# A graph transformer on one core: three low-degree blocks moved to the end of the first layer, one more packing of slots, longer early parts

## The chip, the core and the metric

The kernel runs on one core of a Trainium2 chip. The metric is device time in microseconds of one launch. In the program text the two layers are numbered 0 and 1; the description of the change numbers them 1 and 2, so that its "layer 1" is layer 0 here.

## The reference

Two layers of a typed graph transformer over 6250 nodes of 128 features, 100000 edges, 16 node types and 32 edge types, then a linear map, a residual and a layer norm. Cut to what matters:

```python
def gt_layer(x, ntype, etype, src, dst, Wk, Wq, Wv, Wa, Watt, Wmsg, pri, skip, g, b):
    k, q, v = (typed_linear(x, ntype, W).reshape(n, H, HS) for W in (Wk, Wq, Wv))
    kT = jnp.einsum('nhd,htdo->nhto', k, Watt)      # a row for each node and edge type
    vT = jnp.einsum('nhd,htdo->nhto', v, Wmsg)
    kw, m = kT[src, :, etype], vT[src, :, etype]
    a = jnp.einsum('ehd,ehd->eh', kw, q[dst]) * pri[:, etype].T / SQRT_D
    att = edge_softmax(a, dst, n)
    hag = jax.ops.segment_sum((m * att[:, :, None]).reshape(-1, H * HS), dst, n)
    h = jax.nn.silu(typed_linear(hag, ntype, Wa))
    alpha = jax.nn.sigmoid(skip[ntype])[:, None]
    h = h * alpha + x * (1.0 - alpha)
    return layernorm(h) * g + b
h = x
for l in range(2):
    h = gt_layer(h, ...)                             # weights of layer l
return _layernorm(x + h @ ff_w + ff_b)
```

## The kernel before, in words

**The table.** For each layer the kernel writes a table in HBM with a row for each node and edge type: 32 rows of 256 floats (128 of `kT`, 128 of `vT`) a node. The table of layer 0 is written in the first 600 us. The table of layer 1 is made from the results of layer 0, while layer 0 is still running.

**Blocks and slots.** Nodes are sorted by class (four classes of four node types) and degree, and put 128 at a time, one a partition, into 49 blocks. A block has a width: the number of slots, which is the largest degree that its nodes may have (`OWN` for the eleven blocks of a class, `SHARED` for five blocks that take what is left over from all classes). A **gather** (line 1801, `kv<-tab,ell`) is one indirect DMA on POOL's queue; it brings for each of the 128 nodes the table row of one edge: 128 rows of 1 KB. So a layer costs about as many gathers as its blocks have slots.

**Riding slots.** The last slots of the widest blocks are used by few nodes. Where a slot's upper lanes (partitions) are unused, another slot's few lanes are gathered into them: the rider's indices are copied into the host's index column beforehand, and after the host's gather a small DMA on SP's queue (`kv<-kv`) copies the lanes back down to the rider's own place. A riding slot costs no gather. Before the change a rider and its host lie in the same block.

**Superblocks and visits.** Three or four blocks form a superblock: of each class c, `ca` is the four widest blocks, `cb` the middle four, `cc` the three narrowest; `+a` and `+b` are the shared ones. A visit is the gathers, scores, softmax and sums of one superblock. `ORDERS` gives the order of the visits in each layer. After a visit of layer 0 its **chain** (normalise, typed linear, layer norm, key and value of the next layer) and its **pieces** run beside the gathers of later visits: pieces are the matmuls against the edge weights, the copies into one of three buffers `st`, and the **puts**, one indirect DMA on POOL's queue for each half block (line 2023, `tab<-st,row`), 128 rows of 16 KB, 2.1 MB. A superblock of four blocks has eight puts, one of three has six; layer 1's table takes 98.

**What sets the order.** POOL's instructions stand in the order in which the program emits them. While it emits the gathers, it advances generators by a `tick` a slot: `spread` gives a generator of some steps a rate, so that it ends after a given number of slots. The chain's rate comes from `pace`, that of the pieces from the last lines of `table`. A finished `st` waits some steps and is put when at least three gathers (`APART`) have passed. The other engines' order is set by a scheduler within the data's dependencies.

**Early parts.** Layer 1 cannot gather rows that are not yet put. Its first two visits (the leads, `1a` and `2a`) are therefore split: an early part, whose gathers (`ells` in the names) take only edges whose sources are in superblocks put earlier, and a rest, gathered after the last put. `LATE = (2, 1)` says that the early part of the first lead leaves out the last two superblocks of layer 0's order, and that of the second lead the last one; `EARLY` says how many slots of each block are early. So the first early gather has to see the landing of all puts but those of the last two superblocks, the first of the second lead (before it the pieces of the superblock before the last are rushed to their end) all but those of the last one, and the first gather of the rest has to see the landing of the last put.

**The ring.** Gathers land in a ring of 50 slots; VectorE multiplies and reduces them from there.

## Time and profile before

| what | us |
|---|---|
| time, median of three runs (lowest to highest) | 2882.24 (2880.25 to 2885.86) |
| the profiled execution's own time | 2874.6 |
| its span | 2872.7 |
| first gather of layer 0 / first early gather of layer 1 / first gather of the rest (start) | 595.58 / 1738.71 / 1875.91 |
| last gather / last output write on POOL (start) | 2801.20 / 2864.37 |
| gathers, puts, output writes on POOL | 1620, 98, 49 |

The page of the profile gives each engine's busy time and then the span in 40 equal slices of 71.8 us. The slices up to the eighth are the preparation and layer 0's table, slices 9 to 26 layer 0's edges beside layer 1's table, and those after it layer 1's edges. POOL's busy time is only the issuing of DMAs. The transfers are in the DMA row. In a timeline row the number in brackets is the time that the engine sat idle ahead of the instruction and what ended that idle time.

### The profile page before, as it was taken

What the parts mean: (1) busy time and instruction counts of PE and PEld (TensorE: products, weight loads), DVE (VectorE), ACT (ScalarE), POOL (GpSimd) and SP (SyncE); (2) the same over time, 40 slices, a digit from 0 to 9 for tenths busy, and PEclk for the clock granted to TensorE, in tenths of its full rate; (3) what the DMA queues carried; (4) which work ended last, traced back from release to release, by engine and by line L of the source; (5) the groups of instructions that cost most, each with busy time, mean ns of one, the idle gap of its engine ahead of it and who ended that gap; (6) DMA issues with size and microseconds to landing.
All of it is one profiled execution on the core that took longest, in us unless ns stands there. A gap on an engine that the chain in (4) does not pass through costs nothing. (4 is left out here: it accounts for less than half of the span.)

```text
span 2872.7 us, 22109 instructions
## 1 busy us (share of the span) xinstructions
PE 1729.2 (60%) x5415; PEld 750.8 (26%) x5415; DVE 1856.5 (65%) x4245; ACT 942.6 (33%) x1727; POOL 1979.3 (69%) x2118
## 2 busy tenths in 40 slices
PE   5999889834966886787687787502533433212122
PEld 2445444411322342232233222101212211111010
DVE  8358322247877775767676655747877787666663
ACT  4876655511433433344343454201111111101000
POOL 5333665557777777777777776667777777777776
PEclk9989776655675666677577776555656656555555
DMA  7999999988768777787777899863333333333331
GB/s 220 403 421 373 385 400 405 403 252 209 239 234 281 259 268 249 256 317 272 268 267 263 298 351 357 297 189 104 105 104 104 106 104 105 106 105 105 106 105 50
DMA packets 186099, 678.23 MB, mean 236 GB/s; under 512 B 55586, under 2 KB 101328, under 8 KB 160912
## 3 DMA queue, kind: packets, MB, share of 16 engines
q0 software_dynamic: 113248, 636.05, 62.2%
q1 hardware_dynamic: 66612, 37.21, 4.9%
q10 hardware_dynamic: 6096, 3.43, 0.6%
q8 instruction: 46, 0.75, 0.1%
q14 instruction: 97, 0.79, 0.1%
HBM read 254.44 MB, written 421.89 MB: 235 GB/s over the span
## 5 line engine op out<-in xcount | busy, mean ns | idle before, releaser
L1801 POOL DMA_INDIRECT kv<-tab,ell x1454 | 1386.4, 953 | 470.4 <-issue 370.6
L1817 DVE TENSOR_TENSOR kv<-kv,tb 128x768 f32<-128x768 f32 (+10 forms) x274 | 261.9, 958 | 460.8 <-DMA kv<-tab,ell 301.7
L319 PE MATMUL nb<-xm,weights 128*128 128x384 f32 (+2 forms) x640 | 361.8, 720 | 271.4 <-DVE xm L302 264.2
L361 ACT COPY st<-tb 128x1024 f32<-128x1024 f32 x376 | 368.4, 1012 | 376.7 <-PE tb L377 216.7
L350 ACT COPY st<-tb 128x512 f32<-128x512 f32 x676 | 347.4, 611 | 169.6 <-PE tb L343 90.8
L377 PE MATMUL tb<-bdv,kvT 32*128 32x512 f32 x784 | 284.4, 910 | 122.4 <-ACT st L361 108.4
L377 PE MATMUL tb<-bdk,kvT 32*128 32x512 f32 x784 | 301.0, 915 | 48.6 <-ACT st L361 40.6
L343 PE MATMUL tb<-bdv,vT 32*128 32x512 f32 x784 | 287.6, 803 | 37.7 <-ACT st L350 32.4
L319 PEld LDWEIGHTS nb<-xm,weights 128*128 128x128 f32 x640 | 160.0, 268 | 483.0 <-DVE xm L302 272.6
L1822 DVE TENSOR_REDUCE a<-kv 128x48 f32<-128x768 f32 (+10 forms) x274 | 259.5, 950 | 1.0
L1145 POOL DMA_INDIRECT tab<-st,rows x98 | 101.2, 1033 | 193.1 <-ACT st L350 152.8
L1601 DVE TENSOR_TENSOR tb<-kv,tb 128x512 f32<-128x512 f32 (+7 forms) x407 | 225.7, 555 | 2.0
L343 PE MATMUL tb<-bdk,kT 32*128 32x512 f32 x784 | 213.7, 798 | 1.7 <-DVE last_at L638 1.1
L327 PE MATMUL nb<-ident,hag 128*128 128x128 f32 x98 | 26.5, 414 | 310.3 <-DVE hag L1858 310.3
L1801 POOL DMA_INDIRECT kv<-tab,ells x166 | 159.3, 960 | 69.3 <-issue 44.8
L1590 DVE TENSOR_TENSOR kv<-kv,tb 128x768 f32<-128x768 f32 (+8 forms) x266 | 197.3, 758 | 0.8
L348 DVE COPY st<-tb 128x512 f32<-128x512 f32 x108 | 74.6, 691 | 183.0 <-PE tb L343 99.3
L302 DVE SCALAR_TENSOR_TENSOR xm<-ntb,nb 128x512 f32<-128x512 bf16 (+2 forms) x224 | 126.9, 593 | 49.2 <-PE nb L327 37.3
L343 PEld LDWEIGHTS tb<-bdv,vT 32*128 32x128 f32 x784 | 111.4, 224 | 134.5 <-ACT st L350 111.3
L377 PEld LDWEIGHTS tb<-bdv,kvT 32*128 32x128 f32 x784 | 79.4, 249 | 243.3 <-ACT st L361 185.0
L1574 ACT ACTIVATE tb<-a 128x136 f32<-128x136 f32 (+15 forms) x108 | 30.0, 278 | 312.0 <-DVE a L1572 259.4
L377 PEld LDWEIGHTS tb<-bdk,kvT 32*128 32x128 f32 x784 | 82.6, 249 | 189.0 <-ACT st L361 149.7
(405 smaller groups left out, 2286.6 us busy)
## 6 DMA issues: line engine op xcount, KB each, us to landing
kv<-tab,ell POOLq DMA_INDIRECT x1454
weights<-looks SPq DMA_DIRECT2D x40, 128.0 KB
hr<-xrd SPq DMA_DIRECT2D x16, 256.0 KB
kv<-tab,ells POOLq DMA_INDIRECT x166
xrd<-xr POOLq DMA_DIRECT2D x10, 256.0 KB
weights<-looks SPq DMA_DIRECT2D x40, 64.0 KB
hrd<-hs SPq DMA_DIRECT2D x8, 256.0 KB
hr<-xrd SPq DMA_DIRECT2D x10, 192.0 KB
```

The source lines that it names most:

```text
L302: nc.vector.scalar_tensor_tensor(xm[:, :n], ntb[:, :n], float(t), hT[:, :n], op0=ALU.is_equal, op1=ALU.mult)
L319: nc.tensor.matmul(ps[:, :n], w[:, t, :], xm[:, :n], start=(t == types[0]), stop=(t == types[-1]))
L343: nc.tensor.matmul(pt[:, b], yT[s, i * P:(i + 1) * P], bd[s, tt, :], start=True, stop=True)
L350: nc.scalar.copy(to, pt)
L361: copy(to, pt)
L377: nc.tensor.matmul(pt[:, b], yT[s, i * P:(i + 1) * P], bd[s, tt, :], start=True, stop=True)
L1145: put = nc.gpsimd.indirect_dma_start(out=tabs[0].rearrange("(n t) c -> n (t c)", t=16), out_offset=bass.IndirectOffsetOnAxis(ap=rows1[:, t ...
L1590: nc.vector.tensor_tensor((v_[:, k0:k1] if j or k0 else acc[:, :k1]) .rearrange("p k (h d) -> p k h d", h=H), v_[:, k0:k1].rearrange("p k ...
L1601: nc.vector.tensor_tensor(to, v_, to, op=ALU.add)
L1801: get = nc.gpsimd.indirect_dma_start(out=to.bitcast(I32) if l else to, out_offset=None, in_=tabs[l][:], in_offset=bass.IndirectOffsetOnAxi ...
L1817: nc.vector.tensor_tensor(kk, kk, q[:lanes].unsqueeze(1).to_broadcast([lanes, c, D]), op=ALU.mult)
L1822: nc.vector.tensor_reduce(a[:lanes, j0:j1, :], kk.rearrange("p k (h d) -> p k h d", h=H), axis=AX.X, op=ALU.add)
```

## The change

- Layer 0's order: `2c` (three blocks of 13, 12 and 11 slots) is moved from the ninth place to the last. The last two superblocks are now `0b` and `2c`, where they were `3b` and `0b`. Layer 1's order is the same.
- `EARLY` has 40 and 52 slots, where it had 32 and 44: 92 in all, where there were 76.
- The shared superblock `+b` has widths 16, 15 and 9, where it had 17, 15 and 14, and its three riders may lie in another block than their hosts: `SEATS` lists for each rider the pieces of lanes and where they ride. It gathers 37 slots a layer, where it gathered 40. A rider whose host is in an earlier block takes its place in the ring when the host is gathered (`seat`, `invite`), and waits there for its own block.
- The pieces of the last two superblocks are spread over `TAIL` = 11 slots a block (44 for `0b`, 33 for `2c`), where it was over the 32 and 44 early slots. The last chain but one is no longer sped up to 0.7 of its slots. The rule that spreads the other pieces is unchanged, but it takes the slots of the visit two places later, which is another one now.

```diff
-SHARED = (41, 20, 17, 15, 14)
+SHARED = (41, 20, 16, 15, 9)
-ORDERS = ("1c 3c 1a 1b +a 2a 0c 2b 2c 0a +b 3a 3b 0b",
+ORDERS = ("1c 3c 1a 1b +a 2a 0c 2b 0a +b 3a 3b 0b 2c",
           "1a 2a 0c 3c +b 0b 1c +a 2b 2c 3a 3b 1b 0a")
-EARLY = ((11, 8, 7, 6), (14, 11, 10, 9))
+EARLY = ((13, 10, 9, 8), (16, 13, 12, 11))
+TAIL = 11.0
-OWN_TAILS = {0: ((23, 76, 1, 52),)}
-SHARED_TAILS = {0: ((27, 58, 2, 35), (28, 48, 10, 8)), 2: ((15, 88, 1, 40),),
-                4: ((8, 64, 1, 64), (7, 84, 4, 11))}
+SEATS = {
+    "a": (((0, 24), ((0, 23, 76, 52),)),),
+    "+a": (*(((0, 29 + r), ((0, 27, 58 + 35 * r, 35),)) for r in range(2)),
+           *(((0, 31 + r), ((0, 28, 48 + 8 * r, 8),)) for r in range(10))),
+    "+b": (((1, 14), ((0, 15, 64, 35),)),
+           ((2, 7), ((0, 15, 99, 29), (1, 13, 105, 6), (2, 6, 96, 32))),
+           ((2, 8), ((1, 13, 111, 15),))),
+}
...
             def pace(v):
                 v = min(v, len(visits) - 1)
-                share = 0.7 if 2 < v < n0 else 1.0
+                share = 0.7 if 2 < v < n0 - 1 else 1.0
...
                     spread(pieces, gen, 8 * visits[v][1][1] + (4 if v else 4 + HELP),
-                           (1.0 if v + 4 < n0 else 0.5 if v + 2 < n0 else 1.0) *
-                           slots(min(v + 2, first1 - 1)))
+                           (1.0 if v + 4 < n0 else 0.5) * slots(v + 2) if v + 2 < n0 else
+                           TAIL * visits[v][1][1])
...
+                        def invite():
+
+                            for to in hosting:
+                                awaits[to] = seat(1)
+                                places[to] = awaits[to][1][:, 0, :]
+                            for b2 in range(b, i0 + k):
+                                for slot, (_, pieces) in riders.get(b2, {}).items():
+                                    for at_, n, hb, hs, lane_ in pieces:
+                                        if hb == b:
+                                            nc.sync.dma_start(places[b2, slot][at_:at_ + n],
+                                                              places[b, hs][lane_:lane_ + n])
```

POOL's instructions around the first early gather: before (`st_11536` is the last put of `3a`, `st_11590` and `st_11624` are the first two of `3b`), and now (`st_11600` is the eighth and last of `3b`).

```order
L1801 DMA kv_5794<-tab0_63,ell_77 128x256 x3
L2023 DMA tab1_64<-st_11536,row2_83 12544x4096
L1801 DMA kv_5794<-tab0_63,ell_77 128x256 x4
L2023 DMA tab1_64<-st_11590,row2_83 12544x4096
L1801 DMA kv_5794<-tab0_63,ell_77 128x256 x7
L2023 DMA tab1_64<-st_11624,row2_83 12544x4096
L1801 DMA kv_5794<-tab1_64,ells_5809 128x256 x5
```

```order
L1832 DMA kv_5795<-tab0_63,ell_77 128x256 x3
L2069 DMA tab1_64<-st_11439,row2_83 12544x4096
L2069 DMA tab1_64<-st_11467,row2_83 12544x4096
L1832 DMA kv_5795<-tab0_63,ell_77 128x256 x3
L2069 DMA tab1_64<-st_11498,row2_83 12544x4096
L1832 DMA kv_5795<-tab0_63,ell_77 128x256 x2
L2069 DMA tab1_64<-st_11538,row2_83 12544x4096
L1832 DMA kv_5795<-tab0_63,ell_77 128x256 x3
L2069 DMA tab1_64<-st_11557,row2_83 12544x4096
L1832 DMA kv_5795<-tab0_63,ell_77 128x256 x3
L2069 DMA tab1_64<-st_11600,row2_83 12544x4096
L1832 DMA kv_5795<-tab1_64,ells_5810 128x256 x13
```

The puts of layer 1's table that stand ahead of the early parts have moved closer together, since `3b`'s eight puts now go with the 36 gathers of `2c`, at half of these; and the put whose landing the first early gather has to see is now the instruction just ahead of it. Before, it was `st_11536`, with eleven gathers and two puts in between.

POOL from the end of the first lead's early part to the rest: before (the 17 gathers are the last ten of the first lead and the first seven of the second; `st_11801` is the last put of `3b`, `st_12192` the last of all, and 90 is the rest of both leads), and now (`st_11973` is the last put of `0b`, `st_12176` the last of all, and 88 is 14 early gathers and 74 of the rest).

```order
L2023 DMA tab1_64<-st_11801,row2_83 12544x4096
L1801 DMA kv_5794<-tab1_64,ells_5809 128x256 x17
L2023 DMA tab1_64<-st_11988,row2_83 12544x4096
...
L1801 DMA kv_5794<-tab1_64,ells_5809 128x256 x5
L2023 DMA tab1_64<-st_12192,row2_83 12544x4096
L1801 DMA kv_5794<-tab1_64,ells_5809 128x256 x90
```

```order
L1832 DMA kv_5795<-tab1_64,ells_5810 128x256 x5
L2069 DMA tab1_64<-st_11870,row2_83 12544x4096
L1832 DMA kv_5795<-tab1_64,ells_5810 128x256 x8
L2069 DMA tab1_64<-st_11918,row2_83 12544x4096
L2069 DMA tab1_64<-st_11973,row2_83 12544x4096
L1832 DMA kv_5795<-tab1_64,ells_5810 128x256 x16
L2069 DMA tab1_64<-st_12049,row2_83 12544x4096
...
L1832 DMA kv_5795<-tab1_64,ells_5810 128x256 x3
L2069 DMA tab1_64<-st_12176,row2_83 12544x4096
L1832 DMA kv_5795<-tab1_64,ells_5810 128x256 x88
```

The second lead's first gather (the first of the 16) now stands right behind the two last puts of `0b`, where ten gathers lay in between. Behind the last put of all stand 14 early gathers, where there were none.

More of the change, by code (lines that the diff above doesn't have):

```diff
@@ L147 @@
     OWN0, SHARED0 = CB * P, NC * CB * P
-    def riders(k, groups):
-        out, lanes = [], [P] * k
-        at = max(main for main, _, _, _ in groups) + 1
-        for main, first, n, rest in groups:
-            assert n * rest + first <= P
-            lanes[main] = first
-            for g in range(n):
-                out.append((at, rest, main, first + g * rest))
-                lanes[at] = rest
-                at += 1
-        assert at == k and all(a >= b for a, b in zip(lanes, lanes[1:]))
-        return out, lanes
-    tails = {c * CB + i: riders(OWN[i], g) for c in range(NC) for i, g in OWN_TAILS.items()}
-    tails.update({NC * CB + i: riders(SHARED[i], g) for i, g in SHARED_TAILS.items()})
     holds = slots_for(OWN, BINS, LOW)
@@ L171 @@
             named[f"{c}{part}"] = (c * CB + CB - i0 - k, k, range(c * TC, (c + 1) * TC))
+    riders, lanes_of = {}, {}
+    for name, (i0, k, _) in named.items():
+        seats = SEATS.get(name if name[0] == "+" else name[1], ())
+        if not seats:
+            continue
+        for i in range(k):
+            lanes_of[i0 + i] = [P] * KB[i0 + i]
+        taken = set()
+        for (i, slot), pieces in seats:
+            at, mine = 0, []
+            for hi, hs, lane, n in pieces:
+                assert hi <= i and (hi, hs) not in dict(seats) and lane + n <= P
+                assert taken.isdisjoint((hi, hs, lane + r) for r in range(n))
+                taken.update((hi, hs, lane + r) for r in range(n))
+                of = lanes_of[i0 + hi]
+                of[hs] = min(of[hs], lane)
+                mine.append((at, n, i0 + hi, hs, lane))
+                at += n
+            lanes_of[i0 + i][slot] = at
+            riders.setdefault(i0 + i, {})[slot] = at, mine
+    for b, of in lanes_of.items():
+        assert all(p >= q for p, q in zip(of, of[1:]))
+    hosts = {}
+    for b, of in riders.items():
+        for slot, (_, pieces) in of.items():
+            first = min(hb for _, _, hb, _, _ in pieces)
+            if first < b:
+                hosts.setdefault(first, []).append((b, slot))
     orders = [[named[part] for part in order.split()] for order in ORDERS]
@@ L1739, in edges @@
                     a = ep.tile([P, max(KB), H], F32, name="a")
-                    riding = {} if part else {k: r for k, *r in tails.get(b, ((), ()))[0]}
-                    places, halves = {}, None
-                    bundled = bundles_of(K, riding)
+                    riding = {} if part else riders.get(b, {})
+                    hosting = () if part else hosts.get(b, ())
+                    halves = None
+                    guests = {at[1]: awaits.pop(at) for at in list(awaits) if at[0] == b}
+                    places = {at: held[1][:, 0, :] for at, held in awaits.items()}
+                    bundled, main = bundles_of(K, riding, hosting)
                     stages = [bundled]
@@ L1762, in edges @@
                                     k0, pos = k0 + size, pos + size
-                            bundles += [cut] if riding and len(bundle) > 1 else [[c] for c in cut]
+                            if bundle is main:
+                                pos += len(hosting)
+                                whole.append(len(bundles))
+                            bundles += [cut] if bundle is main else [[c] for c in cut]
                             chunks += cut
```

48 lines of the change are left out of this document (28 added, 20 removed).

## The prediction

> **What bounds the kernel now.** I read the page first, then POOL's groups, its busy time by stretch, its waits, and its timeline around the layers' boundary. The page's busy shares alone don't name the bound; the groups and the stretches do.
>
> ```profile
> PE 1729.2 (60%) x5415; PEld 750.8 (26%) x5415; DVE 1856.5 (65%) x4245; ACT 942.6 (33%) x1727; POOL 1979.3 (69%) x2118
> ```
>
> ```profile
> L1801 POOL DMA_INDIRECT kv<-tab,ell x1454 | 1386.4, 953 | 470.4 <-issue 370.6 <-DMA tab<-st,rows 15.8 <-DMA kv<-tab,ell 11.6
> L1801 POOL DMA_INDIRECT kv<-tab,ells x166 | 159.3, 960 | 69.3 <-issue 44.8 <-DMA tab<-st,row 17.1 <-DMA kv<-tab,ells 2.6
> ...
> L2023 POOL DMA_INDIRECT tab<-st,row x98 | 100.6, 1026 | 36.5 <-issue 20.8 <-ACT st L361 10.6 <-DMA kv<-tab,ell 3.2
> ```
>
> Most of POOL's idle time is "issue", waiting for nothing: each DMA is followed by some 0.30 us before the next. Busy and gap together, POOL is full:
>
> ```profile
> 1600.00:1738.00 138.00, 113.05 (x332) 39.23 (x332) 81.71 (x166) 73.10 (x98) 100.40 (x105) 0.70 0.90 336
> 1738.00:1791.00 53.00, 38.31 (x110) 14.08 (x109) 32.56 (x75) 24.67 (x37) 35.12 (x37) 0.66 0.97 369
> 1791.00:1876.00 85.00, 47.45 (x156) 14.79 (x154) 60.95 (x100) 21.05 (x33) 53.08 (x56) 0.58 0.84 298
> ...
> 2400.00:2500.00 100.00, 31.80 (x71) 14.96 (x71) 66.71 (x153) 11.19 (x28) 75.82 (x80) 0.62 0.37 106
> ```
>
> (Columns: length, then busy time and count of PE, weight load, VectorE, ScalarE, POOL; granted clock, DMA share, GB/s.) In layer 1 there are 80 gathers in 100 us, **1.25 us each**, with the DMA at 0.37 and VectorE at two thirds: the issuing is the bound. A put costs 1.03 + 0.30 = 1.33 us of POOL. From 1600 to 1738 POOL's 100.40 + 105 x 0.30 leave 6.1 us of real stall; from 1738 to 1791 6.8; from 1791 to 1876 15.1. So 28 us of stalls stand where layer 1's table is finished. After that POOL runs on to the end without a break, and so a microsecond saved or lost on POOL anywhere behind 595 us reaches the end one to one:
>
> ```profile
> 2289.84 0.94 POOL L1801 DMA_INDIRECT kv<-tab,ell  x1 [1.41 <-DVE tb L1590]
> ...
> 2801.20 0.95 POOL L1801 DMA_INDIRECT kv<-tab,ell  x1 [0.30 <-issue]
> 2802.45 1.02 POOL L2079 DMA_INDIRECT out_dram<-weights,node  x1 [0.30 <-issue]
> ...
> 2864.37 0.98 POOL L2079 DMA_INDIRECT out_dram<-st,node  x1 [0.30 <-issue]
> ```
>
> The row at 2289.84 is the longest stall that I find after 1876. The stalls before it, in the timeline:
>
> ```profile
> 1636.28 1.02 POOL L2023 DMA_INDIRECT tab<-st,row  x1 [0.30 <-issue]
> ...
> 1647.21 0.94 POOL L1801 DMA_INDIRECT kv<-tab,ell  x1 [1.04 <-DMA tab<-st,row]
> ...
> 1735.38 0.95 POOL L1801 DMA_INDIRECT kv<-tab,ell  x1 [0.30 <-issue]
> 1737.39 1.01 POOL L2023 DMA_INDIRECT tab<-st,row  x1 [1.07 <-DMA kv<-tab,ell]
> 1738.71 1.03 POOL L1801 DMA_INDIRECT kv<-tab,ells  x1 [0.30 <-issue]
> ...
> 1776.26 1.01 POOL L2023 DMA_INDIRECT tab<-st,row  x1 [0.30 <-ACT th L1907]
> ...
> 1790.80 0.94 POOL L1801 DMA_INDIRECT kv<-tab,ells  x1 [4.67 <-DMA tab<-st,row]
> ...
> 1806.56 1.01 POOL L2023 DMA_INDIRECT tab<-st,row  x1 [3.57 <-ACT st L361]
> ...
> 1862.82 1.01 POOL L2023 DMA_INDIRECT tab<-st,row  x1 [0.30 <-issue]
> 1875.91 0.97 POOL L1801 DMA_INDIRECT kv<-tab,ells  x1 [12.08 <-DMA tab<-st,row]
> ```
>
> At 1875.91 the first gather of the rest waits for the last put to land: 12.08 us. The idle at 1647.21 and 1790.80 is on the eighth issue behind the puts at 1636.28 and 1776.26: eight issues last 10 us, and a put that takes longer to land holds up the eighth issue behind it. So puts here land 10.6, 14.2 and 12.8 us after their start (the idle ends about 0.3 us ahead of the gather). The first early gather (1738.71) waits for nothing: the put that it has to see is eleven gathers and two puts back.
>
> ```profile
> 1700.00:1737.00 37.00, 31.73 (x111) 10.75 (x111) 15.13 (x22) 22.93 (x27) 24.28 (x26) 0.78 1.00 391
> 1737.00:1777.00 40.00, 34.22 (x102) 11.48 (x98) 21.14 (x36) 22.22 (x29) 28.54 (x29) 0.69 0.97 377
> 1804.00:1808.00 4.00, 2.63 (x12) 0.52 (x8) 3.88 (x6) 1.44 (x3) 1.14 (x2) 0.50 0.04 16
> 1808.00:1813.00 5.00, 2.46 (x12) 0.89 (x16) 3.85 (x6) 2.02 (x2) 3.78 (x5) 0.50 1.11 410
> ```
>
> Where puts are close together, the DMA engines are full, at 377 to 391 GB/s. The put of 1806.56 met idle engines: its data began to flow 1.4 us after its start, at 410 GB/s.
>
> **The change, part by part.**
>
> *Gathers.* The order has 1614 gathers in place of 1620 (three a layer, all of `+b`), and the same 98 puts and 49 output writes. 6 x 1.25 = **-7.5 us**. On POOL's path this is certain; nothing hides it. The 16 early slots that are added are gathers moved from the rest, and save nothing by themselves.
>
> *Pieces riding in another block.* `+b` now has five such small copies a layer on SP's queue, where it had six. SP takes its queue in order, so behind a copy that waits for its host's gather stand the loads of `hr`, `ntb` and the stores of `hrd`. VectorE waits for a copied slot before the guest's scores. What hides this is the ring: POOL runs up to 50 slots (62 us) ahead of VectorE. I take 0. Only if VectorE fell that far behind would it cost; the row at 2289.84 (1.41 us) is the nearest price, so 0 to +2. The six issues of these copies before were in the same queue, so there is no gain to expect either.
>
> *The dense stretch and the first early gather.* `3b`'s pieces are spread over half the slots of the visit two places later, which is now `2c` with 36 slots, where it was over 32 early slots. In the order 17 puts now stand with only 50 gathers between them, up to the first early gather; the last 17 before had 84. A put is 128 x 4096 floats, 2.10 MB; a gather 128 x 256, 0.13 MB. POOL needs 17 x 1.33 + 50 x 1.25 = 85 us for them. The data, 42.2 MB, need 108 to 112 us at 391 to 377 GB/s; I take 110 (before: 46.6 MB, 121 us against POOL's 128). And the first early gather stands right behind the last of the 17 and has to see it land. Start to landing is thus 110 + 1.4, and the stall 26 us, of which some 12 are at the first early gather (a landing of 13.3, inside 10.6 to 14.2, less the put's own 1.33) and 14 at eighth issues and at puts whose `st` isn't ready. Before, the stretch had 6: **+20 us**. From below: the engines keep up and only the landing is waited for, at the fastest 1.4 + 2.10 MB at 410 GB/s = 6.5 after the start, a wait of 5.2, so -1. From above: PE was busy 65.95 of the 77 us from 1700 to 1777, in which 11 puts were issued: 6.0 us a put with all else that PE does, or 102 us for 17. That is close to the DMA's 110; if PE holds back as it does there (86% busy) the making takes 119, and the term is +31. I take +20, since the row with the DMA at 1.00 is the nearest.
>
> The Trainium skill, "DMA: Bandwidth & Descriptors", section "Specifications", puts the HBM limit for a core at about 358 GB/s. By that the 42.2 MB would need 118 us and the term would be +30. The row above shows 391, which decides.
>
> *Second lead.* Its first gather now stands behind two puts in a row. 4.2 MB at 391 GB/s are 10.7 us; with 1.4 to begin, and less the 2.66 us that the two issues take, the wait is 9.4 where nothing is queued ahead. One put by itself would land in 6.8 by the same sum, and the measured landings are 4 to 7 above it; here eight gathers drain the queue first, so I take 12, and 2 for eighth issues among `0b`'s eight puts. In its place the 6.8 of 1738 to 1791 fall away: **+7 us** (from +2, with 4.2 MB at 410 GB/s, a wait of 9.0 and nothing else, to +12). Behind this waiting gather stand the 15 other gathers and then `2c`'s six puts; VectorE and PE use the wait to catch up.
>
> *End of the early parts.* The first put of `2c` comes after 16 gathers, and its chain has had 40 + 16 gathers, 8 puts and the two waits, over 90 us, where `0b`'s had 71 (1735.38 to 1806.56) and was 3.57 late: that wait goes. Behind the last put are 14 gathers, 17.5 us, more than its landing of 12.8: the wait of 12.08 goes, and an eighth issue may wait some 2. **-13 us** (-15 to -9).
>
> *2c out of the middle.* `2b`'s table is now spread over the slots of `+b`: nine puts stand among 38 gathers, 61 us of data at 391 GB/s against 59 of POOL: **+2 us** (0 to +6).
>
> Sum: -7.5 + 20 + 7 - 13 + 2 = **+8.5 us**. The ends add to -20 and +34 (with the copies' 2). The profiled execution took 2874.6 us (span 2872.7 and 1.9 around it), so its like should take 2883. The median of the runs shown, 2882.24, is 7.6 above that execution; I add to it: **2891 us**.
>
> **The rivals.**
>
> *Puts land fast (faster).* If layer 0's last stretch doesn't fill the DMA engines, the wait at the first early gather is 5.2 and that at the second lead 9.0: -7.5 - 1 + 2 - 13 = -19.5, **2863**. It decides where these two terms, 27 in my sum, together fall below 18.5; below 12.7 it is to be measured. For it: 1806.56, where the data flowed at 410 GB/s. Against it: gathers between 1640 and 1875 waited for puts, which takes a landing of over 10 us (of the eight in this row two are no longer than the usual gap, and one is that of the rest):
>
> ```profile
> POOL kv L1801 <- DMA tab<-st,row: 21.6, 8, 12.1
> ```
>
> Chance 0.19. The Trainium skill, "DMA: Bandwidth & Descriptors", section "Anatomy of one DMA — SWDGE (gpsimd) path", fits a DMA from GpSimd as 2.0 us and its bytes at 436 GB/s; as an estimate a put would land in 6.8 us, this rival's case, and the readings of 10.6 to 14.2 in a full queue differ.
>
> *One backlog, counted once (no change).* The three `st` buffers and the eight open issues take up the dense stretch, no more than 6 us are lost in it, as before, and only the first early gather's 12 are added: -7.5 + 12 + 7 - 13 + 2 = 0.5, **2883**. For it: the four puts from 1745.16 to 1760.65 stood three gathers apart and were issued without a stall:
>
> ```profile
> 1745.16 1.00 POOL L2023 DMA_INDIRECT tab<-st,row  x1 [0.30 <-ACT st L361]
> ...
> 1760.65 1.01 POOL L2023 DMA_INDIRECT tab<-st,row  x1 [0.30 <-issue]
> ```
>
> Against it: 4.67 us came two puts later, at 1790.80. Chance 0.25.
>
> *PE becomes the bound (slower still).* A buffer is refilled only after the put three back has landed (up to 14.2), and pieces of three superblocks and two chains share PE. If the making takes 7.0 us a put, 17 take 119, the last lands some 10 later, and the dense stretch costs 129 - 85 - 6 = +38 in place of +20, in all +26.5, **2909**. It decides from 6.5 us a put on (110 us for 17). For it: PE's 86% from 1700 to 1777. Against it: the longest wait of a put for ScalarE's copies is the 3.57 at 1806.56. Chance 0.15.
>
> *The slow path.* If a node had more edges than its slots, or more late edges than its rest has slots, the kernel would run both layers again by its slow path. Counted on this input's edges: no node exceeds its slots, and the late edges are at most 9, 7, 7, 7 (of 12, 11, 10, 10) and 6, 7, 5, 4 (of 9, 8, 7, 7). Chance 0.01.
>
> **How the numbers follow.** The forecast has 0.40, with 2884 to 2898 as its own range. A change of 0.2%, 5.8 us, is about what can be told from none. Faster by more: the first rival and a little of the second, 0.22. Within: most of the second and the forecast's lower edge, 0.28. Slower: the rest, 0.50. The range from 2868 to 2910 reaches into the first rival and to the third; below it about 0.10 are left, above 0.08.
>
> **What would show it.** Right: the first early gather and the 41st each idle 10 to 14 us behind puts, the first gather of the rest under 1 us; the stall to the first early gather is over 20 us with the DMA at 1.00; 80 gathers in 100 us in layer 1. Wrong: those two waits at 5 us, or the DMA below 0.9 in the dense stretch; or a stall in layer 1 on VectorE behind `kv<-kv`, which my sum holds at nothing.

## The result, and the profile after

The changed kernel takes 2911.89 us (median of four runs, 2906.63 to 2913.66), the kernel before 2883.76 (four runs, 2880.25 to 2885.86): ratio **1.0101**, 95% interval 1.0083 to 1.0118, so 28 us slower. The prediction was 2891 and its range ended at 2910. The profiled execution takes 2906.63 us (span 2904.7), 32.0 more than that of before. All further times are of executions on undisturbed chips, with one exception: in the runs e1 to e5 and e11 to e15 the chip took 3365 to 3387 us for the kernel before, with idle time on PE, ScalarE and VectorE that no row explains, so that of these only ratios are given and nothing rests on them.

POOL's groups after the change, and how POOL's waits between 1300 and 1950 us divide (the second fence: total, times, longest):

```profile
L1832 POOL DMA_INDIRECT kv<-tab,ell x1448 | 1382.2, 955 | 473.6 <-issue 373.1 <-DMA tab<-st,rows 15.6 <-DMA kv<-tab,ell 12.7
L2069 POOL DMA_INDIRECT tab<-st,row x98 | 100.7, 1028 | 69.9 <-ACT st L379 39.1 <-issue 18.6 <-ACT tb L1593 4.2
```

```profile
POOL kv L1832 <- issue: 120.9, 342, 8.5
POOL tab L2069 <- ACT st L379: 37.3, 17, 6.7
```

A gather and a put cost POOL what they did, 0.955 and 1.028 us. What is new is the second row of the waits: puts wait 37 us for ScalarE's copies into `st`, where all puts of before waited 10.6. The long waits for a landing are put down to "issue" (most of these 342 are gaps of 0.30 us, and two are of over 8). In POOL's timeline the stalls stand in four places:

```profile
1397.65 1.02 POOL L2069 DMA_INDIRECT tab<-st,row  x1 [6.70 <-ACT st L379]
1420.58 1.01 POOL L2069 DMA_INDIRECT tab<-st,row  x1 [2.94 <-ACT st L379]
...
1740.16 0.99 POOL L2069 DMA_INDIRECT tab<-st,row  x1 [6.71 <-ACT st L379]
1746.54 1.02 POOL L2069 DMA_INDIRECT tab<-st,row  x1 [1.54 <-ACT tb L1561]
...
1752.91 1.01 POOL L2069 DMA_INDIRECT tab<-st,row  x1 [2.37 <-ACT st L379]
...
1759.29 1.02 POOL L2069 DMA_INDIRECT tab<-st,row  x1 [1.59 <-ACT st L379]
...
1775.88 1.03 POOL L1832 DMA_INDIRECT kv<-tab,ells  x1 [8.38 <-issue]
...
1853.28 1.04 POOL L1832 DMA_INDIRECT kv<-tab,ells  x1 [8.47 <-issue]
...
1919.97 0.94 POOL L1832 DMA_INDIRECT kv<-tab,ells  x1 [2.00 <-DMA tab<-st,row]
...
2319.29 0.94 POOL L1832 DMA_INDIRECT kv<-tab,ell  x1 [3.13 <-DVE kv L1609]
...
2335.20 0.94 POOL L1832 DMA_INDIRECT kv<-tab,ell  x1 [2.47 <-DVE tb L1609]
```

`2b`'s puts (1397 to 1434), the dense stretch with the first early gather (1775.88), the second lead (the 41st early gather, 1853.28), and two gathers of layer 1. In the dense stretch the last puts follow each other at 6.4 us (1740.16, 1746.54, 1752.91, 1759.29), each waiting for its copies. The stretches (length, then busy time and count of PE, weight load, VectorE, ScalarE and POOL; granted clock, DMA share, GB/s), with two short ones of different clock and one of layer 1:

```profile
1380.00:1440.00 60.00, 50.20 (x140) 18.56 (x137) 32.40 (x71) 26.29 (x33) 36.17 (x38) 0.70 0.91 336
1668.00:1776.00 108.00, 94.49 (x274) 31.80 (x268) 48.98 (x100) 60.22 (x74) 56.47 (x60) 0.66 0.95 366
1682.00:1706.00 24.00, 18.31 (x75) 5.49 (x73) 8.60 (x16) 15.58 (x19) 14.35 (x15) 0.93 0.95 372
1730.00:1770.00 40.00, 38.00 (x99) 12.90 (x96) 16.34 (x44) 23.24 (x29) 18.14 (x19) 0.51 0.96 368
1776.00:1860.00 84.00, 65.22 (x216) 23.90 (x216) 45.13 (x95) 42.35 (x60) 51.65 (x54) 0.70 0.80 294
...
2400.00:2500.00 100.00, 27.47 (x70) 13.71 (x68) 67.22 (x169) 12.64 (x36) 75.76 (x80) 0.59 0.36 104
```

A row's stall is its length less POOL's busy time and 0.30 us for each of its instructions: 12.4 us in the middle, 33.5 ahead of the first early gather, 16.2 from there to the second lead. The kernel before has none in the same 60 us (60 - 45.68 - 48 x 0.30), which the change filled with `2b`'s puts:

```profile
1380.00:1440.00 60.00, 39.24 (x85) 13.27 (x86) 35.83 (x82) 18.31 (x27) 45.68 (x48) 0.59 0.78 271
```

In the dense stretch two things are nearly full at once, PE (94.49 of 108 us) and the DMA engines (0.95). The clock that PE is granted there is 0.93 from 1682 to 1706 and 0.51 from 1730 to 1770, and PE's share goes from 76% to 95%. A matmul of the pieces takes 587 ns at the fastest and 1218 at the slowest (the second fence is PE's timeline), and a group of eight, of which a put needs two, 2.18 us busy early in the stretch and 3.56 late in it, where one group follows the other after 3.19:

```profile
L395 PE MATMUL tb<-bdk,kvT x128: 587/894/1218, 1660.4 to 1780.0; 32*128 32x512 f32 x128
L395 PE MATMUL tb<-bdv,kvT x120: 587/1056/1218, 1666.4 to 1777.7; 32*128 32x512 f32 x120
```

```profile
1702.23 2.18 PE L395 MATMUL tb<-bdk,kvT 32*128 32x512 f32 x8 [0.47 <-ACT st L379]
...
1738.46 3.56 PE L395 MATMUL tb<-bdk,kvT 32*128 32x512 f32 x8 [0.98 <-ACT st L379]
...
1741.65 3.56 PE L395 MATMUL tb<-bdv,kvT 32*128 32x512 f32 x8
```

At the end of the early parts the stall is gone but for 2.00 us (1919.97).

### The profile page after: what moved, and what is told of

Read it like the earlier page. It is cut to its first block, busy times and chain, and to the rows that moved or that the text cites. A ratio compares the mean times of both kernels' runs of the same rounds, so it can differ in the third digit from the quotient of the medians.

```text
span 2904.7 us, 22074 instructions
## 1 busy us (share of the span) xinstructions
PE 1752.5 (60%) x5415; PEld 759.0 (26%) x5415; DVE 1843.9 (63%) x4240; ACT 945.8 (33%) x1731; POOL 1976.0 (68%) x2112
## 4 chain that ended last, share of the span: by engine, by line
DVE 15%; POOL 10%; issue 9%; DMA 9%; PE 7%; ACT 1%; DVEq 0%; POOLq 0%; SPq 0%; ACTq 0%
POOL kv L1832 9%; DMA kv<-tab,ell 5%; PE tb L395 3%; DVE kv L1863 3%; DVE tb L1620 2%; DMA tab<-st,row 2%; PE nb L337 2%; DVE kv L1609 2%; DVE a L1868 2%; DVE xm L320 1%; POOL out_dram L2125 1%; DMA kv<-tab,ells 1%; PE nb L345 1%; DVE tb L1609 1%; DVE sums L1625 1%
## 5 line engine op out<-in xcount | busy, mean ns | idle before, releaser
L1863 DVE TENSOR_TENSOR kv<-kv,tb 128x768 f32<-128x768 f32 (+6 forms) x273 | 260.0, 955 | 492.1 <-DMA kv<-tab,ell 314.7
L337 PE MATMUL nb<-xm,weights 128*128 128x512 f32 (+2 forms) x640 | 367.6, 728 | 258.0 <-DVE xm L320 255.3
L1868 DVE TENSOR_REDUCE a<-kv 128x48 f32<-128x768 f32 (+6 forms) x273 | 258.1, 948 | 1.1
L1620 DVE TENSOR_TENSOR tb<-kv,tb 128x512 f32<-128x512 f32 (+4 forms) x407 | 224.6, 552 | 1.9
L1609 DVE TENSOR_TENSOR kv<-kv,tb 128x768 f32<-128x768 f32 (+9 forms) x266 | 195.9, 752 | 0.8
L2069 POOL DMA_INDIRECT tab<-st,row x98 | 100.7, 1028 | 69.9 <-ACT st L379 39.1
L1593 ACT ACTIVATE tb<-a 128x96 f32<-128x96 f32 (+15 forms) x108 | 29.9, 277 | 328.4 <-DVE a L1591 256.6
## 6 DMA issues: line engine op xcount, KB each, us to landing
xrd<-xr POOLq DMA_DIRECT2D x10, 256.0 KB, 12.4
```

Of the source, the lines that this page charges most:

```text
L337: nc.tensor.matmul(ps[:, :n], w[:, t, :], xm[:, :n], start=(t == types[0]), stop=(t == types[-1]))
L1609: nc.vector.tensor_tensor((v_[:, k0:k1] if j or k0 else acc[:, :k1]) .rearrange("p k (h d) -> p k h d", h=H), v_[:, k0:k1].rearrange("p k ...
L1620: nc.vector.tensor_tensor(to, v_, to, op=ALU.add)
L1863: nc.vector.tensor_tensor(kk, kk, q[:lanes].unsqueeze(1).to_broadcast([lanes, c, D]), op=ALU.mult)
L1868: nc.vector.tensor_reduce(a[:lanes, j0:j1, :], kk.rearrange("p k (h d) -> p k h d", h=H), axis=AX.X, op=ALU.add)
```

## The experiments

The theories: **A**, the new order of layer 0 loses the time, since POOL has to wait for puts; **B**, the new packing or the longer early parts do. Under A it had to be found what makes the puts late: the DMA engines (**E**), PE's matmuls (**F**), or the turns between PE, ScalarE and the `st` buffers (**G**); and whether the wait at the first early gather is a loss of its own (**C**) or a debt that shows elsewhere if it is taken away there (**D**).

In this table POOL's stall is worked out as above, from stretches laid at the same puts (60 us over `2b`'s puts, the 108 us up to the first early gather, and from there to the first gather of the second lead, the 41st, in e8 the 33rd). Each row is one profiled execution.

| kernel | median us | middle | dense stretch | to second lead |
|---|---|---|---|---|
| changed kernel | 2911.9 | 12.4 | 33.5 | 16.2 |
| e18, the same as control | 2912.1 | 11.8 | 33.4 | 16.0 |
| e8, new order alone | 2929.6 | 7.3 | 39.0 | 18.8 |
| e6, half of each put's bytes | 2930.2 | 11.7 | 38.9 | 25.7 |
| e10, every second matmul of the pieces | 2938.5 | 18.8 | 43.5 | 17.2 |
| e16, half of the pieces' groups of matmuls | 2898.7 | 5.2 | 29.0 | 15.6 |
| e17, no wait for `3b`'s puts at the first lead | 2906.5 | 8.9 | 25.0 | 16.2 |

In the middle the first two rows and e17 run the same instructions, and have 12.4, 11.8 and 8.9: a difference of 3.5 us there is no more than one execution's scatter.

### The parts of the change: e8, e9, e7

The new order alone, in the kernel before (e8; e2 was the same kernel):

```diff
-ORDERS = ("1c 3c 1a 1b +a 2a 0c 2b 2c 0a +b 3a 3b 0b",
+ORDERS = ("1c 3c 1a 1b +a 2a 0c 2b 0a +b 3a 3b 0b 2c",
```

> The kernel before with one edit: in layer 0, 2c stands last in place of behind 2b. Packing, early slots, spread and pace are the old ones. Theory A: it loses what the changed kernel's trace shows in layer 0 without the gains of the rest: middle +13, dense stretch and first early gather +28, second lead +5, and the end wait of 12 us stays: 2884 + 46 = about 2929 us, and above 2915 in any case. Theory B: the order costs less than half of that, below 2905 us, and the rest of the loss comes from the packing or the added early slots.

> The kernel of e2 again (the kernel before with one edit: 2c last in layer 0). Theory A: middle +13, dense stretch and first early gather +28, second lead +5, and the wait of 12 us at the end of the early parts stays: about 2929 us, above 2915 in any case. Theory B: less than half of that, below 2905 us.

Measured 2929.64 us beside 2882.96: ratio 1.0153, 1.0123 to 1.0183 (e2: 1.0171, 1.0122 to 1.022). Theory A's number, and its places; the waits at the first early gather, the first of the second lead (the 33rd here, since `EARLY` is that of before) and the first gather of the rest:

```profile
1782.16 1.03 POOL L1801 DMA_INDIRECT kv<-tab,ells  x1 [9.12 <-DVE sums L1606]
...
1852.17 1.02 POOL L1801 DMA_INDIRECT kv<-tab,ells  x1 [10.86 <-DMA tab<-st,row]
...
1926.81 0.97 POOL L1801 DMA_INDIRECT kv<-tab,ells  x1 [11.41 <-DMA tab<-st,row]
```

So the order costs 44 us by the ratio and 47 by the medians, and the rest of the change gives 15 to 18 of it back, of which 9.4 are the third wait (11.41 to 2.00) and 7.5 the gathers.

The packing alone, with the order, the early slots, the spread and the pace of before (e9; e1 the same; the lines of the spread and the pace are left out here):

```diff
-ORDERS = ("1c 3c 1a 1b +a 2a 0c 2b 0a +b 3a 3b 0b 2c",
+ORDERS = ("1c 3c 1a 1b +a 2a 0c 2b 2c 0a +b 3a 3b 0b",
-EARLY = ((13, 10, 9, 8), (16, 13, 12, 11))
+EARLY = ((11, 8, 7, 6), (14, 11, 10, 9))
...
```

> The changed kernel with the packing alone (the third shared superblock's blocks of 16, 15 and 9 slots and the riders' seats); order of layer 0, number of early slots, spread and pace are those of the kernel before. Theory A (the loss is the new order of layer 0: puts crowded in front of the first early gather and in the middle): six gathers fewer by 1.25 us and nothing else, 7.5 us below the kernel before, about 2876 us. Theory B (the riders in other blocks cost: VectorE waits for a copied slot, the ring runs dry, gathers of layer 1 wait for VectorE as in the 3.13 and 2.47 us of the changed kernel's trace): the saving is eaten up, 2882 us or more.

> The kernel of e1 again (the changed kernel's packing alone). Theory A: six gathers by 1.25 us less, about 2876 us. Theory B (riders in other blocks cost as much as the gathers save): 2882 us or more.

Measured 2882.8 beside 2882.96: ratio 0.9993, 0.9973 to 1.0013 (e1: 1.0058, 1.003 to 1.0085). That is theory B's number: the gain of 7.5 us isn't there. Two places of POOL's timeline have more stall than before:

```profile
1812.87 1.02 POOL L2069 DMA_INDIRECT tab<-st,row  x1 [8.00 <-ACT st L379]
...
2294.90 0.94 POOL L1832 DMA_INDIRECT kv<-tab,ell  x1 [3.07 <-DVE kv L1609]
...
2310.90 0.94 POOL L1832 DMA_INDIRECT kv<-tab,ell  x1 [2.49 <-DVE tb L1609]
```

The first is the put that waited 3.57 us before (+4.4). The other two are the waits for VectorE in layer 1, which come at the same gathers, of the same length, in the changed kernel too (3.13 and 2.47). Less 0.30 of issue each they are 5.0 us of stall. The kernel before had the row at 2289.84 that the prediction shows (1.41) and two more, 1.8 in all:

```profile
2304.14 0.94 POOL L1801 DMA_INDIRECT kv<-tab,ell  x1 [0.85 <-DVE tb L1590]
2309.32 0.94 POOL L1801 DMA_INDIRECT kv<-tab,ell  x1 [0.48 <-DVE tb L1601]
```

VectorE's timeline shows it waiting for `+a`'s slots just ahead, in e9 14.72 us and before 12.32. What ends the wait is a gather in e9 and a rider's copy (`kv<-kv`) before; which step of the new seating makes it longer isn't shown:

```profile
2289.57 1.22 DVE L1863 TENSOR_TENSOR kv<-kv,tb 128x1024 f32<-128x1024 f32 x1 [14.72 <-DMA kv<-tab,ell]
```

```profile
2285.98 1.22 DVE L1817 TENSOR_TENSOR kv<-kv,tb 128x1024 f32<-128x1024 f32 x1 [12.32 <-DMA kv<-kv]
```

Together +4.4 and +3.2 are about the 7.5. The second goes with the packing: it comes back in e7, in the changed kernel and in the control, and not in e8, which has the old packing (two waits, of 1.29 and 1.31). That the first is the packing's too isn't shown (one execution, and the interval spans 11 us; at 1790.80, where the kernel before stalls 4.67, e9 doesn't, and it has a new wait of 4.33 at 1723.23).

All of the change but the order (e7; e3 and e5 the same): the first line of the diff above alone.

> The changed kernel with the old order of layer 0 (2c behind 2b); packing, 92 early slots, spread and pace are those of the changed kernel. Theory A: the saving of 7.5 us and part of the waits at the end of the early parts (five more early gathers behind the last put, 6 us of its 12 us wait), about 2884 - 7.5 - 6 = 2870 us, between 2865 and 2876. Theory B (packing or the longer early part costs by itself): 2882 us or more.

> The kernel of e3 again (the changed kernel with the old order of layer 0), since in e1 to e4 the chip ran the kernel before at 3376 us in place of 2884, with waits for nothing and for other queues on PE, VectorE and ScalarE that cover what was to be told apart. Theory A (the loss is the new order of layer 0): 2884 - 7.5 - 6 = about 2870 us, between 2865 and 2876. Theory B (packing or the longer early part costs by itself): 2882 us or more. On a chip that runs the kernel before at another time: 14 us below it, or not below it.

> The kernel of e3 and e5 a third time (the changed kernel with the old order of layer 0: 2c behind 2b; packing, 92 early slots, spread and pace kept), on a chip that ran the kernel before at 2886 us in e6. Theory A (the loss is the new order of layer 0): 2884 - 7.5 - 6 = about 2870 us, between 2865 and 2876. Theory B (packing or the longer early part costs by itself): 2882 us or more.

Measured 2886.89: ratio 1.0014, 0.9995 to 1.0034 (e3: 1.0074, 1.0038 to 1.011; e5 was too scattered, 3391 to 4499 us). That is theory B's number (2882 or more) and 17 us above A's. So each theory has a part of it: the order is the loss (e8), and without the order the rest of the change gives nothing.

```profile
1821.65 1.04 POOL L1832 DMA_INDIRECT kv<-tab,ells  x1 [12.53 <-DMA tab<-st,row]
...
1905.37 0.94 POOL L1832 DMA_INDIRECT kv<-tab,ells  x1 [7.34 <-DMA tab<-st,row]
```

The new spread puts the last two puts of `3b` right ahead of the second lead here too, whose wait (12.53) takes the place of what the longer early part saves at the end (12.08 to 7.34). It is the second-lead term of the prediction, seen by itself.

### What makes the puts late: e6, e10, e16

Half of each put's bytes (e6). Half of layer 1's table is left unwritten, and layer 1 reads the other table:

```diff
-                                    out=to.bitcast(I32) if l else to, out_offset=None, in_=tabs[l][:],
+                                    out=to, out_offset=None, in_=tabs[0][:],
...
-                    out=tabs[1].rearrange("(n t) c -> n (t c)", t=16),
+                    out=tabs[1].rearrange("(n t) c -> n (t c)", t=8 if fast else 16),
...
-                    in_=st.rearrange("p t c -> p (t c)").bitcast(I32), in_offset=None,
+                    in_=st.rearrange("p t c -> p (t c)")[:, :2048 if fast else 4096].bitcast(I32),
+                    in_offset=None,
```

> The changed kernel with every put of layer 1's table at half its bytes (2048 of the 4096 columns of a row pair), so half of table 1 is left unwritten; layer 1's gathers read table 0 in its place, and the order of all instructions is as in the changed kernel. Theory E (the DMA engines bound the dense stretch and 2b's puts: st buffers come free only as puts land): the stalls in front of the first early gather, 34 us there, fall to some 5, those in the middle from 13 to 3, those at the second lead from 16 to 8: about 47 us less than the changed kernel, 2865 us. Theory F (PE and ScalarE bound them, with three superblocks' pieces and two chains on PE): only the two waits for a landing (8.4 and 8.5 us) shrink, by 3 to 4 us each, and the puts wait for ScalarE's copies as long as before: about 2903 us.

Measured 2930.18 (two runs) beside 2886.03: ratio 1.0154, 1.0078 to 1.023. Neither number comes, E's 2865 nor F's 2903.

```profile
1679.00:1787.00 108.00, 94.97 (x260) 32.96 (x261) 46.83 (x99) 59.12 (x72) 52.94 (x54) 0.61 0.53 191
```

```profile
POOL tab L2069 <- ACT st L379: 67.6, 23, 9.8
```

```profile
1787.28 1.03 POOL L1832 DMA_INDIRECT kv<-tab,ells  x1 [4.66 <-issue]
...
1873.99 1.04 POOL L1832 DMA_INDIRECT kv<-tab,ells  x1 [4.37 <-issue]
```

The DMA engines fell to 0.53 and the two landings to half (4.66 and 4.37 for 8.38 and 8.47). But the puts wait for their copies 67.6 us in place of 37.3, and the dense stretch has 5 us more stall, not 29 less. Theory E falls: with the DMA engines half idle the puts come no sooner. In that stretch ScalarE's copies wait 26.4 us for PE's matmuls and not once for a landing. That the puts come later than in the changed kernel goes with a lower granted clock, 0.61 for 0.66; what lowered it isn't known.

Every second matmul of the pieces left out (e10, but for the first put of each superblock), so half of the columns of layer 1's table hold what stood in PSUM:

```diff
-                            nc.tensor.matmul(pt[:, b], yT[s, i * P:(i + 1) * P], bd[s, tt, :],
-                                             start=True, stop=True)
+                            if not b or not i and not tg:
+                                nc.tensor.matmul(pt[:, b], yT[s, i * P:(i + 1) * P], bd[s, tt, :],
+                                                 start=True, stop=True)
```

> The changed kernel without every second matmul of the pieces of layer 1's table (128 of a superblock's 256 or so), so half of the columns of that table hold what stood in PSUM before; ScalarE's copies, the puts with all their bytes and the order are as in the changed kernel. Theory F (PE bounds the making of the pieces, since halved puts in e6 took the DMA from 0.95 to 0.55 in the dense stretch and the puts waited for ScalarE's copies as long as before): the waits of puts for ScalarE's copies fall from some 50 us between 1300 and 1900 us to under 15, eighth issues and the two landings wait as before or up to 6 us more; about 30 us less than the changed kernel, 2882 us. Theory G (ScalarE's own copies, 1.0 us each and eight for a put, or VectorE's share of the chains bound it): no more than 10 us less, 2902 us or more.

Measured 2938.5 (two runs): ratio 1.0182, 1.014 to 1.0224. Slower, with half of the matmuls. By its number alone that would be theory G (2902 or more), but PE's timeline of e10 tells why it decides nothing between F and G:

```profile
1701.75 3.15 PE L396 MATMUL tb<-bdk,kvT 32*128 32x512 f32 x4
1704.92 3.15 PE L396 MATMUL tb<-bdv,kvT 32*128 32x512 f32 x4
1708.09 3.15 PE L396 MATMUL tb<-bdk,kvT 32*128 32x512 f32 x4
```

```profile
1700.00:1732.00 32.00, 31.84 (x53) 10.46 (x52) 15.71 (x28) 21.18 (x24) 22.90 (x25) 0.52 0.97 374
```

Four matmuls take 3.17 us from start to start at a clock of 0.52. In the changed kernel eight, in the pairs that the program makes of two slices of 32 rows, take 3.19 at 0.51 (1738.46 and 1741.65 above): the two of a pair run beside each other, and to leave out one of each saves PE nothing. The Trainium skill says the same of matmuls in different row strips ("TensorE: Matmul & The Clock Gate", "Part 3: Packing small matmuls"). Why e10 is slower than the changed kernel, by 23 us (ratios) to 27 (medians), stays open; its granted clock is lower over the whole run (0.649 for 0.659).

So whole groups, the second half of each piece, were left out instead (e16; e11 and e13 the same kernel). The columns that hold messages aren't computed, again but for each superblock's first put:

```diff
-                            nc.tensor.matmul(pt[:, b], yT[s, i * P:(i + 1) * P], bd[s, tt, :],
-                                             start=True, stop=True)
+                            if not half or not i and not tg:
+                                nc.tensor.matmul(pt[:, b], yT[s, i * P:(i + 1) * P], bd[s, tt, :],
+                                                 start=True, stop=True)
```

> The changed kernel without the matmuls of the second half of each piece (the columns that hold messages, 8 of a put's 16 matmuls), so those columns of layer 1's table hold what stood in PSUM; ScalarE's copies, the puts with all their bytes and the order are as in the changed kernel. In e10 every second matmul was left out, which left PE as busy (98.2 of 108 us in the dense stretch): a group of 4 took 3.15 us there where the 8 of the changed kernel take 3.4 to 3.56 at the same granted clock of 0.50, so it didn't halve PE's time and told nothing. Here whole groups fall away, and PE's time for a put falls from 7.1 to 3.6 us at that clock. Theory F (PE bounds the making): then the DMA engines are next, 2.10 MB at 391 GB/s or 5.4 us a put: the dense stretch loses 34 - 17 x 0.9 = some 19 us in place of 34, the middle 3 in place of 13, the second lead 11 in place of 16: 30 us less than the changed kernel, about 2882 us, and the puts' waits for ScalarE's copies before the first early gather are under 10 us. Theory G (the turns between PE, ScalarE and the st buffers bound it, whoever computes): less than 10 us, 2902 us or more.

> The kernel of e11 again: the changed kernel without the second half of each piece's matmuls (the columns that hold messages), copies and puts as they were. Theory F (PE bounds the making): the DMA engines are next, 2.10 MB at 391 GB/s or 5.4 us a put: the dense stretch loses some 19 us in place of 34, the middle 3 in place of 13, the second lead 11 in place of 16: 30 us less than the changed kernel, about 2882 us. Theory G (the turns between PE, ScalarE and the st buffers bound it, whoever computes): 2902 us or more.

> The kernel of e11 and e13 again: the changed kernel without the second half of each piece's matmuls (the columns that hold messages), copies and puts as they were, now beside the changed kernel on the same chip. Theory F (PE bounds the making): 30 us less than the control, at least 20, and the waits of puts for ScalarE's copies halved or less. Theory G (the turns between PE, ScalarE and the st buffers, whoever computes): less than 10 us from the control.

Measured 2898.7 beside the control's 2912.06 on the same chip, 13 us less: ratio to before 1.0052, 1.0028 to 1.0077, the control's 1.0102, 1.0064 to 1.0141 (e11 0.9907, 0.9876 to 0.9937; e13 0.9943, 0.991 to 0.9976). Waits, timeline and stretches:

```profile
POOL tab L2070 <- ACT st L379: 13.9, 5, 6.1
```

```profile
1764.03 1.02 POOL L1833 DMA_INDIRECT kv<-tab,ells  x1 [10.98 <-issue]
...
1811.62 0.94 POOL L1833 DMA_INDIRECT kv<-tab,ells  x1 [3.93 <-DMA tab<-st,row]
...
1840.86 1.04 POOL L1833 DMA_INDIRECT kv<-tab,ells  x1 [10.71 <-issue]
```

```profile
1375.00:1435.00 60.00, 44.33 (x126) 18.44 (x126) 42.40 (x102) 30.08 (x42) 41.92 (x43) 0.74 1.00 380
1656.00:1764.00 108.00, 75.58 (x208) 26.14 (x208) 52.72 (x108) 68.50 (x87) 60.14 (x63) 0.66 0.97 382
```

The puts' waits for copies fall from 36.3 (control) to 13.9: F's sign, against G, under which the turns would have kept them. But only 13 of the 30 us come, between the two theories' numbers. In the middle the stall falls from 12 to 5. In the dense stretch it falls by 4 only: the DMA engines are at 0.97 and 382 GB/s, and the landings rise to 10.98 and 10.71. What ScalarE's copies wait for in this stretch has changed as well (a buffer `st` is free again only when its put has landed):

```profile
ACT st L379 <- DMA tab<-st,row: 17.6, 4, 9.5
ACT st L379 <- PE tb L396: 11.0, 10, 3.8
```

In the changed kernel's 108 us these two are 5.0 for landings and 23.6 for PE. **There are two limits of nearly the same height.** Take the bytes away and PE holds the copies, and so the puts; take PE's work away and the landing holds the copies and the gathers. In the middle PE seems to be most of the limit; in the dense stretch neither is the limit alone.

### The wait at the first early gather: e17, beside the control e18

The first lead leaves out the last three superblocks' edges in place of two, so that its first gather needs `0a`, `+b` and `3a` and not `3b`; the order is unchanged (e4, e12 and e14 the same kernel: 1.0107, 1.0093 and 1.0117).

```diff
-LATE = (2, 1)
+LATE = (3, 1)
```

> The changed kernel with one number changed: the first lead's early gathers leave out the edges of the last three superblocks' rows in place of the last two's, so that the first early gather no longer has to see 3b's puts landed. The instructions stand in the same order. Theory C (the wait of 8.4 us at the first early gather is a loss of its own): 8 us less than the changed kernel, about 2904 us. Theory D (the DMA engines are full there, and whatever doesn't wait at this gather waits at the next puts and at the eighth issues behind them): 2909 to 2912 us, no difference that can be measured.

> The kernel of e4 again (the changed kernel, its first early gather no longer waiting for 3b's puts, same order). Theory C (the 8.4 us of that wait are a loss of their own): 2904 us. Theory D (the making is behind: what doesn't wait at this gather waits at the puts and eighth issues that follow): 2909 to 2912 us, no difference that can be measured.

> The kernel of e4 and e12 again (the changed kernel, its first early gather no longer waiting for 3b's puts, same order). Theory C (the 8.4 us of that wait are a loss of their own): 2904 us. Theory D (the making is behind: what doesn't wait at this gather waits at the puts and eighth issues that follow): 2909 to 2912 us, no difference that can be measured.

> The kernel of e4, e12 and e14 again (the changed kernel, its first early gather no longer waiting for 3b's puts, same order), beside the control. Theory C (the 8.4 us of that wait are a loss of their own): 8 us less than the control. Theory D (the making is behind, and what doesn't wait at this gather waits at the puts and eighth issues that follow): within 3 us of it.

> The changed kernel itself, without an edit: the control for e16 and e17. Where the chip runs the kernel before at 2884 us, 2912 us (28 us more); on a chip that takes 3365 to 3390 us for the kernel before, 34 us more, as e4, e12 and e14 did with the first early gather's wait taken away.

Measured 2906.54 beside the control's 2912.06: 5.5 us less, ratios 1.0079 (1.0056 to 1.0103) and 1.0102 (1.0064 to 1.0141), which the intervals don't separate. The trace does:

```profile
1765.46 1.02 POOL L2069 DMA_INDIRECT tab<-st,row  x1 [2.42 <-ACT st L379]
1766.78 1.03 POOL L1832 DMA_INDIRECT kv<-tab,ells  x1 [0.30 <-issue]
```

```profile
1659.00:1767.00 108.00, 94.51 (x270) 31.99 (x271) 48.64 (x99) 62.91 (x77) 63.16 (x66) 0.62 0.95 368
```

The wait at the first early gather is gone, the stretch has 8.4 us less stall, its other long waits are those of the control to 0.3 us, and the stretch behind it has as much as the control (16.2 and 16.0). In the trace theory C holds; the time, 5.5 us less, lies between C's 8 and D's 3. The control repeats the changed kernel, in time and in each of the three stretches to 1 us.

### `2b`'s puts spread wider: e15

```diff
-                           (1.0 if v + 4 < n0 else 0.5) * slots(v + 2) if v + 2 < n0 else
+                           (1.6 if v == 7 else 1.0 if v + 4 < n0 else 0.5) * slots(v + 2) if v + 2 < n0 else
```

> The changed kernel with one number changed: 2b's puts are spread over 1.6 times the slots of +b in place of once, so that nine puts stand among some 60 gathers and not among 38, and 0a's puts move back by as much. Theory F (PE makes a put in 6.4 us where its clock is 0.50, and the stretch of +b asked for one every 6.6 us with its chains on PE beside it): the stalls of the middle fall from 13 us to 3, and nothing is paid later, since 0a's puts have 74 gathers: 2902 us. Rival (the debt of pieces moves on to the dense stretch, since the sum of PE's work is the same): 2909 us or more.

Ratio 1.0142, 1.0079 to 1.0204, beside 1.0117 for the kernel of e17 on the same chip (e14). No gain is to be seen, but the changed kernel itself didn't run there: not conclusive.

## Why the prediction was wrong

The direction was right, and every place where time was lost or won had a term; the size was not. Term by term, from the two profiled executions:

| step | predicted | measured |
|---|---|---|
| gathers, 1620 to 1614 | -7.5 | -7.5 (1448 + 166 gathers, 1.25 each) |
| riders in another block | 0 (0 to +2) | +3 (5.0 of stall in layer 1, before 1.8) |
| dense stretch and first early gather | +20 (-1 to +31) | +27.5 (33.5, before 6) |
| second lead | +7 (+2 to +12) | +9.4 (16.2, before 6.8) |
| end of the early parts | -13 | -13.4 (15.1 less the 1.7 left) |
| `2c` out of the middle | +2 (0 to +6) | +12 (12.4, before none) |
| sum | +8.5 | +31, beside 32.0 |

**The step that failed is the pricing of making.** "*2c out of the middle*" set nine puts, "61 us of data at 391 GB/s against 59 of POOL", and stopped there: it never asked what has to be computed before nine puts. PE is busy 50.20 of 60 us there at a clock of 0.70, and the puts wait for copies. The longest wait (6.70, at 1397.65) follows right behind sixteen matmuls of a chain, which PE did ahead of the pieces' next ones:

```profile
1384.54 9.82 PE L2020 MATMUL nb<-xm,weights 128*128 128x512 f32 x16
```

The control has the same pair (10.10 us, then a wait of 5.35). In e16 the sixteen take 10.14 us too, and no put waits behind them. The second wait (2.94, at 1420.58) isn't PE's: ScalarE's copies stand there behind a small copy that waits 5.73 us for VectorE's sums (1418.18). e6 (half of the bytes) leaves the middle's stall at 11.7, and e16 (half of the pieces' matmuls) brings it to 5.2, 3.7 below the least of the three executions with all of them (8.9 in e17), which scatter by 3.5. So the greater part of the middle seems to be PE's, for pieces and a chain together, and 10 of the missing 23 us are here, above the bound of +6 that the prediction gave.

"*The dense stretch*" was priced by the data alone, 110 us for 17 puts, and PE by 6.0 us a put "close to the DMA's 110"; that was put into the upper bound (+31), where the result lies. With PE relieved (e16) the stretch has 29.0 us of stall, +23 for the predicted +20: as a price by the landings the term was nearly right. With PE as it is, it is 27.5. The 6.0 us a put were an average over clocks, though the rows they came from had 0.78 and 0.69. At 0.50 a put takes 6.4 (1746.54 to 1759.29), and the clock is 0.51 from 1730 to 1770. The third rival, PE as the bound "from 6.5 us a put on", had the mechanism and gave 2909. That this is 3 us from the result is luck: its price was too high for the dense stretch (+38 for 27.5), and it didn't see the middle (+2 for 12).

"*Second lead*" and "*End of the early parts*" held in their numbers. The landing that the prediction took as 12 us of wait is 8.4 to 8.5 at both gathers, so a put lands 9.1 us after its start (1766.48 to 1775.88 and 1843.83 to 1853.28, less the usual 0.3), below the 10.6 to 14.2 of before; an eighth issue and late copies (puts waiting 3.34 and 4.22 us, at 1818.60 and 1843.83) made up for it. Of what was named to show it right, a stall above 20 us and 80 gathers in 100 us in layer 1 came true; the waits of 10 to 14 us didn't, nor the DMA at 1.00 (0.95), nor the first gather of the rest under 1 us (2.00).

"*Pieces riding in another block*" was taken at 0 (at most +2) because the ring runs 50 slots ahead. The "stall in layer 1 on VectorE", named as what would make the prediction wrong, is there, with +3. Of the **rivals**, "puts land fast" needed its two terms together below 18.5, and they are 36.9; "one backlog, counted once" allowed the dense stretch 6 us besides the first early gather's wait, and it has 25 (25.0 in e17, where that gather waits for nothing). "The slow path" would have run both layers again, and the trace has 1614 gathers. Two of the prediction's sums are off, with no effect on its number: the lower ends add to -21.5 and not -20, and 118 us of data would make the dense stretch's term +28 and not +30.

## What to carry to other kernels

Where one queue feeds itself (gathers of a table that is still being written), price each stretch for every producer in the chain, at the clock that the stretch grants and not at the mean: here a put needed 5.4 us of DMA and 4.4 to 6.4 of PE, and the one that wasn't priced for the middle set most of it. Two limits of nearly the same height can't be told by taking one away; take away each, and expect only a part of its price back (here none for the bytes and 13 of 30 us for PE's work). And a move that unloads the end of a pipeline should be tried alone, before the edits that are to pay for it.

## What the runs showed of the hardware

PE's granted clock in these stretches goes between 1.00 (1390 to 1410 us) and 0.50 (1730 to 1750) within tens of microseconds, and a matmul of the pieces takes 587 to 1218 ns. How busy PE is doesn't tell it: PE is busy 18.38 of 20 us at the 1.00, 38.00 of 40 at 0.51 in the row of 1730 to 1770 above, and 10.22 of 30 at 0.50 from 1860 to 1890. The Trainium skill ("TensorE: Matmul & The Clock Gate", "Part 1: The HAM clock gate") has the same two values, but lets some 3.4 us of sustained activity lift the clock to the full; by that these 40 us would have run at 1.00, and the measurement decides. Nor did less work lift it: with half of the pieces' groups gone (e16) the mean over the profiled execution is 0.645, with every second matmul gone (e10) 0.649, in the control 0.655. What the gate counts as activity, these runs don't show.
